# Starting a group's expert layer beside the dispatch of its second sequence, at a fixed pace

## The chip, the cores and the metric

The kernel runs on one core of one Trainium2 chip. The metric is the device time of one execution in microseconds (us), the median of the runs. TensorE is PE in the profile, its weight loads PEld, VectorE DVE, ScalarE ACT, GpSimd POOL and SyncE SP.

## The reference

The input is 16 sequences of 512 positions with 256 channels, all in fp32. Two layers follow each other, each with a residual and a layer norm.

The first layer is a selective state-space layer that runs in both directions. Each sequence is projected to 512 inner channels, convolved over 4 positions, and gives step sizes `dt` and, for each of 16 states, rows B and C. Per state and channel a running sum over the positions follows:

```
dA_cum = exp(reverse cumulative sum of dt * A)
xs = cumsum(dt * u * B * dA_cum) / (dA_cum + 1e-12)
y = sum over the 16 states of xs * C,  plus u * D
```

The two directions are added, gated by silu of a second projection, and projected back to 256 channels.

The second layer is a soft mixture of 16 experts with 64 slots each, 1024 slots in all:

```
logits = layernorm(x) @ slot embeddings
slots  = softmax over the positions (dispatch), applied to layernorm(x)
eout   = (gelu(slots @ Wg + bg) * (slots @ Wu + bu)) @ Wd + bd     for each expert
out    = softmax over all slots (combine), applied to eout
```

An expert's weights are three matrices of 512 KB.

## The kernel before, in words

**The scan sets the beat.** The loop at L1048 goes over the 16 sequences `b`. For each it calls `scan_part` four times (forward and backward, for two pairs of channel blocks of 128). A `scan_part` walks over the states in twos and, for each, over two channel blocks: 16 steps, so 64 steps for a sequence. A step has this work:

- POOL multiplies `du` by the B rows into `db` (L442), and at the end `hg` by the C rows `cs` (L471).
- ACT makes the decays `h` (L459) and the factors `th` (L461).
- DVE runs the scan (L465, L467) and joins it with `th` into `hg` (L470).
- PE adds `hg` up over the states by transposing it into the PSUM tile `acc` (L386), two steps later (`add_up`).

`hg` has four buffers, the rows `bs` and `cs` three; SP loads them. Some states, chosen by `diag_of`, let PE make `db` instead (`hd`, L420): four of 16 in the sequences 0 to 2, two of 16 after.

**Side work is threaded between the steps.** Everything else is written as Python generators, which hand out *pieces*: a few matmuls into one or two of three PSUM banks (`BANKS`), then, a step later, what empties the bank. There are three queues of generators, objects of the class `Side`:

- `prep` prepares the next scan part (projections, convolution, `dt`, transposes).
- `front` runs `finish(b)`: output projection, residual and layer norm of a finished sequence, then its `dispatch` (logits `pl`, softmax, transposes `pd`, slots `pq`, `sl`). Slots go to HBM (`s_dram`) in four quarters; `dispatched[b]` counts them.
- `back` runs `experts(g, 0, 8)` and then `combine` for both sequences of group `g`, the sequences 2g and 2g+1. `experts` works in eight pairs of experts, each pair on the slots of both sequences: the load `st<-s_dram`, gate matmuls `pg`, up `pu`, down `peo`, and the store `e_dram<-eo`. `combine` works in four blocks of 128 positions: logits again (`cl`), softmax, transposes (`ctp`), and `cpo`.

After each step `beside_scan` lets `prep` put in a piece, then `front` and `back` by credit:

```
            def paced_piece(self, gaps):
                self.credit = min(self.credit + sum(x[0] for x in self.gens) / max(self.left, 1), 2.0)
                self.left -= 1
                if self.credit >= 1.0 and self.piece(gaps):
                    self.credit -= 1.0
```

So a queue's pace is its pieces that remain by the steps that remain. `experts` already waits at each pair until its quarter of the second sequence's slots is there (`while not ready(ep): yield WAIT`); where the group starts late, it never has to.

**When a group starts.** In an odd sequence `b` from 3 on, the group g = (b - 3) / 2 joins `back`: both of its sequences were dispatched by then. It has 128 steps, the rest of this sequence and the next; group 6 joins in sequence 15 and has 64. In sequence 15 (`hurry`) pieces may follow each other without a gap. Group 7 has no scan beside it: after the last step comes a tail, in which `side_by_side` runs the last `finish`, what is left of `back`, and group 7, with eight PSUM banks.

The order within an engine is not always that of the source: the framework schedules by priority, and `late` pins an instruction to the program's order.

Of the kernel before, what the change touches and what calls it, by code (L numbers as in the profile page):

```python
# [55 lines left out]
def seq_layers(tc, ident, neghalf, a, out):  # L56
# [21 lines left out]
    nb = a["x"].shape[0]  # L78
    with ExitStack() as ctx:
# [200 lines left out]
        def diag_of(b):  # L280

            return (3, 7, 11, 15) if b < 3 else (5, 13)
# [124 lines left out]
        def scan_part(b, r, p, v, accs, done, then):  # L407

            prep.drain()
            prep.gens += [[1, g] for g in [turn_pair(b, r, p, v)] + then]  # L410
            w, ds = side[r], diag_of(b)
            made = {}

            def by_diagonal(n, c):

                diags.append(count[0])
                made[n, c] = h = bank(f"hd_{b}_{r}_{n}_{c}")
                for lc in range(NL):
                    s = slice(lc * P, (lc + 1) * P)
                    ins = nc.tensor.matmul(h[:, s], v[c][3][:, s], dg[:, s], start=True, stop=True)  # L420
                    if lc == 0:
                        late(ins)

            chunks = (2 * p, 2 * p + 1)
            for n in range(0, NS, 2):
                q = f"{b}_{r}_{p}_{n}"
                k = 1 if n + 1 in ds else 2

                bs = p4.tile([P, 2, L], F32, tag="bs", name=f"bs_{q}")
                cs = p4.tile([P, 2, L], F32, tag="cs", name=f"cs_{q}")  # L430
                nc.sync.dma_start(bs[:, :k, :], v["bc"][0, n : n + k, :].unsqueeze(0).to_broadcast([P, k, L]))
                nc.sync.dma_start(cs, v["bc"][1, n : n + 2, :].unsqueeze(0).to_broadcast([P, 2, L]))
                if n + 3 in ds:
                    dg = p4.tile([P, L], F32, tag="dg", name=f"dg_{q}", bufs=1)
                    nc.sync.dma_start(
                        dg.rearrange("p (l s) -> p l s", l=NL),
                        diag_dram[r, ds.index(n + 3), :, : P * P].rearrange("l (p s) -> p l s", p=P),
                    )
                for c in chunks:
                    dt, rr, du = v[c][:3]  # L440
                    db = p4.tile([P, 2, L], F32, tag="db", name=f"db_{q}_{c}")
                    nc.gpsimd.tensor_tensor(  # L442
                        db[:, :k, :], du.unsqueeze(1).to_broadcast([P, k, L]), bs[:, :k, :], ALU.mult
                    )
                    hg = p4.tile([P, 2, L], F32, tag="hg", name=f"hg_{q}_{c}", bufs=4)
                    hs = {}
                    for j in range(2):
                        if j < k:
                            dec = h = ps_h.tile([P, L], F32, tag="h", name=f"h_{q}_{c}_{j}")
                            hs[j] = (h, dec, db[:, j, :])  # L450
                        else:
                            h = made.pop((n + j, c))
                            dec = p4.tile([P, L], F32, tag="dec", name=f"dec_{q}_{c}", bufs=2)
                            hs[j] = (h, dec, h)

                    ths = {}
                    for j in range(2) if k == 2 else (1, 0):
                        s = slice(n + j, n + j + 1)
                        nc.scalar.activation(hs[j][1], dt, AF.Exp, scale=w["A"][:, c, s])  # L459
                        ths[j] = p4.tile([P, L], F32, tag="th", name=f"th_{q}_{c}_{j}")  # L460
                        nc.scalar.activation(ths[j], rr, AF.Tanh, bias=LN_1E12 / 2, scale=w["Ah"][:, c, s])  # L461
                    for j in range(2):
                        (h, dec, add), th = hs[j], ths[j]
                        if r == 0:
                            nc.vector.tensor_tensor_scan(h, dec, add, 0.0, ALU.mult, ALU.add)  # L465
                        else:
                            nc.vector.tensor_tensor_scan(  # L467
                                h[:, ::-1], dec[:, ::-1], add[:, ::-1], 0.0, ALU.mult, ALU.add
                            )
                        nc.vector.scalar_tensor_tensor(hg[:, j, :], th, 1.0, h, ALU.add, ALU.mult)  # L470
                    nc.gpsimd.tensor_tensor(hg, hg, cs, ALU.mult)  # L471
                    pending.append(
                        (r == n == 0, n == 0, r == 1 and n == NS - 2, c, hg, accs, w, v["u"], f"acc_{q}_{c}", done)
                    )
                    evict()

                    nxt_n = n if c == chunks[0] else n + 2
                    if nxt_n + 1 in ds:
                        for x in sides:
                            x.take_up()  # L480
                        by_diagonal(nxt_n + 1, chunks[1] if c == chunks[0] else chunks[0])
                    beside_scan()
                    if k == 1:
                        diags.pop(0)
                    add_up(2)

        class Side:


            def __init__(self):  # L490
                self.gens, self.hold, self.need, self.left, self.credit = [], None, 0, 0, 0.0
                self.wait = self.took = self.gap = False

            def add(self, steps, gen):
                self.gens.append([steps, gen])

            def begin(self, scan_steps):
                self.left, self.credit = scan_steps, 0.0
# [20 lines left out]
            def piece(self, gaps=True):  # L519

                done = False
                while self.gens and self.hold is None and not self.wait:
                    if self.gap and self.took and gaps:
                        break
                    oldest = min([x.hold for x in sides if x.hold is not None] + diags[:1], default=count[0])
                    if count[0] - oldest + self.need > BANKS:
                        break
                    done = True
                    head = self.gens[0]
                    head[0] = max(head[0] - 1, 1)  # L530
                    fresh = len(head) == 2
                    if fresh:
                        head.append(True)
                    self.go()
                    if not fresh and (not self.gens or self.gens[0] is head):
                        break
                return done

            def paced_piece(self, gaps):
                self.credit = min(self.credit + sum(x[0] for x in self.gens) / max(self.left, 1), 2.0)  # L540
                self.left -= 1
                if self.credit >= 1.0 and self.piece(gaps):
                    self.credit -= 1.0

            def drain(self):
                while self.gens:
# [4 lines left out]
        hurry = False  # L551
        diags = []

        prep, front, back = sides = [Side(), Side(), Side()]
# [480 lines left out]
                yield WAIT  # L1035
                put(0, NL, *both)

        FINISH, COMBINE, PAIR = 32, 14, 4
        fwd = {}
        prep.add(1, prep_forward(0, 0, ND, fwd))  # L1040
        prep.drain()
# [6 lines left out]
        for b in range(nb):  # L1048
            bwd, nxt, accs = {}, {}, {}

            if b >= 3 and b % 2 == 1:
                g = (b - 3) // 2
                back.add(8 * PAIR, experts(g, 0, 8))
                back.add(COMBINE, combine(2 * g))
                back.add(COMBINE, combine(2 * g + 1))
            hurry = b + 1 == nb
            front.begin(64)
            back.begin(128 if b % 2 == 1 and b + 1 < nb else 64)

            def gate(c, b=b, accs=accs, bwd=bwd):  # L1060
                y = bwd["res"]
                late(nc.vector.tensor_tensor(y[:, c, :], y[:, c, :], accs[c], ALU.mult))
                if c == ND - 1:
                    front.add(FINISH, finish(b, y))

            scan_part(
                b, 0, 0, fwd, accs, None, [turn_back(b, fwd, bwd), prep_backward(b, bwd), prep_pair(b, 1, 0, bwd)]
            )
            scan_part(b, 1, 0, bwd, accs, gate, [prep_gate(b, fwd, bwd), prep_pair(b, 0, 1, fwd)])
            then = [prep_pair(b, 1, 1, bwd)]  # L1070
            if b + 1 < nb:
                then.append(prep_forward(b + 1, 0, 2, nxt))
            scan_part(b, 0, 1, fwd, accs, None, then)
            then = [prep_forward(b + 1, 2, ND, nxt), prep_pair(b + 1, 0, 0, nxt)] if b + 1 < nb else []
            scan_part(b, 1, 1, bwd, accs, gate, then)
            front.drain()
            fwd = nxt
# [16 lines left out]
        g, kept = nb // 2 - 1, {}  # L1094
# [52 lines left out]
```

## Time and profile before

| what | value |
|---|---|
| median of 3 runs | 5326.35 us (5323.48 to 5327.91) |
| the profiled execution | 5322.25 us, its span 5320.5 us |
| mean granted PE clock | 0.897 |
| sequences 1 and 2 | 283.3 and 285.6 us |
| sequences 3 and 4 | 321.5 and 308.5 us |
| sequences 9 and 10 | 327.0 and 307.9 us |
| sequence 15 | 370.3 us |
| after the last step | 240.5 us |
| `s_dram<-sl`, issue to landing | 3.9 us |
| `st<-s_dram`, issue to landing | 4.2 us |

A sequence's time is taken from its first L471 product to the next sequence's first, and read with the stage windows. The odd sequences from 5 to 13 are alike, and so are the even ones from 4 to 14. The busy time of an engine is an average over stages with different limits, so it is read within one stage.

### The profile page before, as it was taken

What the parts mean: (1) busy time and instruction counts of PE and PEld (TensorE: products, weight loads), DVE (VectorE), ACT (ScalarE), POOL (GpSimd) and SP (SyncE); (2) the same over time, 40 slices, a digit from 0 to 9 for tenths busy, and PEclk for the clock granted to TensorE, in tenths of its full rate; (3) what the DMA queues carried; (4) which work ended last, traced back from release to release, by engine and by line L of the source; (5) the groups of instructions that cost most, each with busy time, mean ns of one, the idle gap of its engine ahead of it and who ended that gap; (6) DMA issues with size and microseconds to landing.
All of it is one profiled execution on the core that took longest, in us unless ns stands there. A gap on an engine that the chain in (4) does not pass through costs nothing. (4 is left out here: it accounts for less than half of the span.)

```text
span 5320.5 us, 74550 instructions
## 1 busy us (share of the span) xinstructions
PE 4310.4 (81%) x24498; PEld 3411.1 (64%) x24498; DVE 4560.6 (86%) x6284; ACT 4104.9 (77%) x6573; POOL 4681.6 (88%) x2537
## 2 busy tenths in 40 slices
PE   5677776897778978788788878889787897878889
PEld 3556565676567756676666766667666676657667
DVE  7999999889998899888898888988898889987733
ACT  6777878887888877888887887888778887777644
POOL 6999999989999899999999989998999989988710
PEclk7778888998899989999899988899888998889999
DMA  5444444675446644576446754467544664447545
GB/s 141 137 129 152 126 142 131 211 234 152 146 146 224 222 144 143 171 226 206 132 140 198 236 169 151 134 210 230 157 151 144 217 227 149 144 153 230 168 135 168
DMA packets 614820, 907.82 MB, mean 171 GB/s; under 512 B 84606, under 2 KB 404734, under 8 KB 614432
## 3 DMA queue, kind: packets, MB, share of 16 engines
q1 hardware_dynamic: 532740, 859.35, 50.9%
q10 hardware_dynamic: 81692, 43.70, 3.1%
q8 instruction: 195, 3.19, 0.2%
q14 instruction: 193, 1.58, 0.1%
HBM read 840.34 MB, written 62.56 MB: 170 GB/s over the span
## 5 line engine op out<-in xcount | busy, mean ns | idle before, releaser
L471 POOL TENSOR_TENSOR hg<-hg,cs 128x1024 f32<-128x1024 f32 x1024 | 2416.9, 2364 | 125.0 <-DVE hg L470 108.0
L442 POOL TENSOR_TENSOR db<-du,bs 128x1024 f32<-128x1024 f32 (+1 forms) x1024 | 2087.7, 2042 | 227.8 <-DVE h L465 84.1
L470 DVE SCALAR_TENSOR_TENSOR hg<-th,h 128x512 f32<-128x512 f32 x1744 | 1156.8, 679 | 183.4 <-PE acc L386 105.9
L386 PE MATMUL acc<-ident,hg 128*128 128x128 f32 x8192 | 1163.6, 292 | 106.4 <-POOL hg L471 84.6
L386 PEld LDWEIGHTS acc<-ident,hg 128*128 128x128 f32 x8192 | 1034.4, 152 | 284.6 <-POOL hg L471 131.3
L467 DVE TENSOR_TENSOR_SCAN h<-h,db 128x512 f32<-128x512 f32 x872 | 1044.9, 1219 | 104.9 <-ACT h L459 92.6
L465 DVE TENSOR_TENSOR_SCAN h<-h,db 128x512 f32<-128x512 f32 x872 | 1044.1, 1219 | 44.5 <-ACT h L459 43.6
L461 ACT ACTIVATE th<-rr,Ah_f 128x512 f32<-128x512 f32 x1024 | 724.6, 714 | 200.9 <-DVE hg L470 198.1
L461 ACT ACTIVATE th<-rr,Ah_b 128x512 f32<-128x512 f32 x1024 | 721.3, 712 | 153.5 <-DVE hg L470 143.5
L459 ACT ACTIVATE h<-dt,A_f 128x512 f32<-128x512 f32 x872 | 591.4, 680 | 99.5 <-DVE hg L470 96.3
L459 ACT ACTIVATE h<-dt,A_b 128x512 f32<-128x512 f32 x872 | 592.3, 680 | 85.6 <-DVE hg L470 81.7
L420 PE MATMUL hd<-dg,duT 128*128 128x128 f32 x2432 | 375.7, 305 | 73.2 <-ACT duT L364 27.1
L420 PEld LDWEIGHTS hd<-dg,duT 128*128 128x128 f32 x2432 | 347.9, 220 | 84.5 <-ACT duT L364 29.5
L710 PE MATMUL pl<-x2T,seT 128*128 128x512 f32 x512 | 294.1, 704 | 78.4 <-DVE hg L470 37.4
L838 PE MATMUL peo<-Wd,ht 128*128 128x256 f32 x1024 | 258.1, 408 | 63.2 <-DVE rr L346 36.6
L869 PEld LDWEIGHTS pg<-st,Wg 128*128 128x128 f32 x2048 | 243.1, 195 | 94.1 <-issue 82.8
L811 PE MATMUL pu<-st,Wu 128*128 128x128 f32 x2048 | 255.6, 284 | 49.3 <-DMA Wu<-in_Wu_dram 27.0
L1015 PE MATMUL cpo<-ceo,ct 128*128 128x256 f32 x1024 | 256.0, 407 | 43.2 <-DVE rr L346 40.0
L811 PEld LDWEIGHTS pu<-st,Wu 128*128 128x128 f32 x2048 | 245.9, 199 | 60.6 <-DVE h L467 29.5
L838 PEld LDWEIGHTS peo<-Wd,ht 128*128 128x128 f32 x1024 | 205.5, 206 | 106.1 <-DVE rr L346 39.2
L869 PE MATMUL pg<-st,Wg 128*128 128x128 f32 x2048 | 265.0, 284 | 4.5 <-DMA st<-s_dram 3.4
L1015 PEld LDWEIGHTS cpo<-ceo,ct 128*128 128x128 f32 x1024 | 207.2, 207 | 87.2 <-DVE rr L346 42.7
(165 smaller groups left out, 6754.0 us busy)
## 6 DMA issues: line engine op xcount, KB each, us to landing
cs<-bc SPq DMA_DIRECT2D x512, 512.0 KB, 3.9
bs<-bc SPq DMA_DIRECT2D x360, 512.0 KB, 5.2
Wg<-in_Wg_dram SPq DMA_DIRECT2D x128, 512.0 KB, 5.7
Wu<-in_Wu_dram SPq DMA_DIRECT2D x128, 512.0 KB, 5.8
Wd<-in_Wd_dram SPq DMA_DIRECT2D x128, 512.0 KB, 5.5
dg<-diag_dram SPq DMA_DIRECT2D x152, 256.0 KB, 4.3
bs<-bc SPq DMA_DIRECT2D x152, 256.0 KB, 3.5
x<-in_x_dram SPq DMA_DIRECT2D x32, 512.0 KB, 6.5
```

Of the source, the lines that this page charges most:

```text
L386: ins = nc.tensor.matmul(accs[c][:, s], hc[:, j, s], ident, is_transpose=True, start=False, stop=(last and j == 1 and lc == NL - 1),)
L420: ins = nc.tensor.matmul(h[:, s], v[c][3][:, s], dg[:, s], start=True, stop=True)
L442: nc.gpsimd.tensor_tensor(db[:, :k, :], du.unsqueeze(1).to_broadcast([P, k, L]), bs[:, :k, :], ALU.mult)
L459: nc.scalar.activation(hs[j][1], dt, AF.Exp, scale=w["A"][:, c, s])
L461: nc.scalar.activation(ths[j], rr, AF.Tanh, bias=LN_1E12 / 2, scale=w["Ah"][:, c, s])
L465: nc.vector.tensor_tensor_scan(h, dec, add, 0.0, ALU.mult, ALU.add)
L467: nc.vector.tensor_tensor_scan(h[:, ::-1], dec[:, ::-1], add[:, ::-1], 0.0, ALU.mult, ALU.add)
L470: nc.vector.scalar_tensor_tensor(hg[:, j, :], th, 1.0, h, ALU.add, ALU.mult)
L471: nc.gpsimd.tensor_tensor(hg, hg, cs, ALU.mult)
L811: nc.tensor.matmul(pu[:, fc * P : (fc + 1) * P], got["Wu", e][:, k, fc * P : (fc + 1) * P], st[:, k, :, j * SL : (j + 1) * SL], start=(k = ...
L838: nc.tensor.matmul(po[:, j * DM : (j + 1) * DM], ht[:, fc, :], got["Wd", e0 + j][:, fc, :], start=(fc == 0), stop=(fc == NF - 1),)
L869: nc.tensor.matmul(pg[:, fc * P : (fc + 1) * P], got["Wg", e][:, k, fc * P : (fc + 1) * P], st[:, k, :, j * SL : (j + 1) * SL], start=(not ...
```

## The change

A group joins `back` one sequence earlier, in the even sequence b = 2g + 2, while the dispatch of its second sequence (2g + 1) runs in `front`. The pairs start as the quarters of the slots are written. The pace of `back` is no longer worked out from what remains: it is 0.5 credits a step (`rate`), and a piece costs 1.1 credits in `experts` and 0.8 in `combine` (`weight`, the third entry of a generator's record). In the last sequence the old rule is put back, with 64 steps to go. Group 6 so starts in sequence 14, and group 7 is run in the tail as before. `diag_of` is not changed.

```diff
             def __init__(self):
+                self.rate = None
...
-            def add(self, steps, gen):
-                self.gens.append([steps, gen])
+            def add(self, pieces, gen, weight=1.0):
+                self.gens.append([pieces, gen, weight])
...
-                    fresh = len(head) == 2
+                    fresh = len(head) == 3
...
             def paced_piece(self, gaps):
-                self.credit = min(self.credit + sum(x[0] for x in self.gens) / max(self.left, 1), 2.0)
+                rate = self.rate or sum(x[0] for x in self.gens) / max(self.left, 1)
+                self.credit = min(self.credit + rate, 2.0)
                 self.left -= 1
+                weight = self.gens[0][2] if self.gens else 0.0
                 if self.credit >= 1.0 and self.piece(gaps):
-                    self.credit -= 1.0
+                    self.credit -= weight
...
-        FINISH, COMBINE, PAIR = 32, 14, 4
+
+        FINISH, COMBINE, EXPERTS = 32, (13, 0.8), (25, 1.1)
+        back.rate = 0.5
...
-            if b >= 3 and b % 2 == 1:
-                g = (b - 3) // 2
-                back.add(8 * PAIR, experts(g, 0, 8))
-                back.add(COMBINE, combine(2 * g))
-                back.add(COMBINE, combine(2 * g + 1))
+            if b >= 2 and b % 2 == 0:
+                g = b // 2 - 1
+                back.add(EXPERTS[0], experts(g, 0, 8), EXPERTS[1])
+                for i in range(2):
+                    back.add(COMBINE[0], combine(2 * g + i), COMBINE[1])
             hurry = b + 1 == nb
             front.begin(64)
-            back.begin(128 if b % 2 == 1 and b + 1 < nb else 64)
+            if hurry:
+                back.rate = None
+                back.begin(64)
```

More of the change, by code (lines that the diff above doesn't have):

```diff
@@ L409, in scan_part @@
             prep.drain()
-            prep.gens += [[1, g] for g in [turn_pair(b, r, p, v)] + then]
+            prep.gens += [[1, g, 1.0] for g in [turn_pair(b, r, p, v)] + then]
             w, ds = side[r], diag_of(b)
```

## The prediction

> **What bounds the kernel now.** I read the page first: no engine is near full over the whole span, and the page's chain of waits covers only the last few per cent, so the span has to be cut by sequence. Each sequence makes 64 `hg`-by-`cs` products on POOL (L471), so the first product of each marks its start; the stage windows between those marks are the next view.
>
> ```profile
> PE 4310.4 (81%) x24498; PEld 3411.1 (64%) x24498; DVE 4560.6 (86%) x6284; ACT 4104.9 (77%) x6573; POOL 4681.6 (88%) x2537
> ...
> core 0: us, PE busy (x) PEld busy (x) DVE busy (x) ACT busy (x) POOL busy (x), PEclk, DMA share, GB/s
> ...
> 619.20:762.40 143.20, 102.51 (x601) 84.11 (x600) 131.61 (x165) 112.24 (x180) 139.46 (x81) 0.82 0.44 135
> 762.40:904.80 142.40, 100.42 (x567) 80.00 (x566) 132.27 (x162) 116.76 (x186) 138.35 (x74) 0.84 0.43 138
> ...
> 2804.50:2968.20 163.70, 133.67 (x842) 112.35 (x839) 140.24 (x195) 131.69 (x201) 150.09 (x85) 0.92 0.65 206
> 2968.20:3131.50 163.30, 149.91 (x899) 118.31 (x899) 143.91 (x204) 129.84 (x198) 145.21 (x73) 0.97 0.69 222
> 3131.50:3286.10 154.60, 118.09 (x639) 92.20 (x639) 142.25 (x195) 124.84 (x209) 148.31 (x81) 0.86 0.45 139
> 3286.10:3439.40 153.30, 125.77 (x642) 92.42 (x641) 139.76 (x191) 123.74 (x209) 146.80 (x77) 0.91 0.44 142
> 4709.70:4898.90 189.20, 156.91 (x964) 128.36 (x961) 145.91 (x212) 143.16 (x213) 150.33 (x85) 0.90 0.65 206
> 4898.90:5080.00 181.10, 154.63 (x867) 121.48 (x868) 137.06 (x203) 121.84 (x204) 135.29 (x67) 0.95 0.52 166
> 5080.00:5320.50 240.50, 216.87 (x1216) 177.37 (x1215) 71.71 (x199) 97.36 (x210) 14.78 (x45) 0.97 0.52 160
> ```
>
> The rows are the halves of sequences 2, 9, 10 and 15, then the tail. Sequence 2, with no experts or combine beside it, is POOL's (278 us busy of 286). Sequence 9 has a whole group's experts (16, run as eight pairs): POOL works 295 us of 327. Sequence 10 has that group's combine (eight blocks of 128 rows): the same POOL work in 308 us. So experts cost about 9 us more per half than combine does. Sequence 15 has all of group 6's experts and most of its combine in its own 64 steps: 370 us, with less POOL work (286 us). How POOL is held up there is in the waits of its second half, and in the timeline of the tail's start, where TensorE is the busy engine:
>
> ```profile
> POOL hg L471 <- DVE hg L470: 26.4, 14, 4.6
> PEld ctp L954 <- ACT cm L947: 20.6, 9, 6.6
> PE ctp L954 <- ACT cm L947: 17.8, 5, 6.4
> DVE hg L470 <- PE acc L386: 11.8, 8, 4.8
> ...
> 5114.25 3.60 PE L933 MATMUL cl<-seT,cx 128*128 128x512 f32 x8
> 5119.63 1.32 PE L954 MATMUL ctp<-ident,cm 128*128 128x128 f32 x8 [1.79 <-ACT cm L947]
> 5120.79 0.60 PE L686 MATMUL px<-ident,xn 128*128 128x128 f32 x4
> 5121.23 3.66 PE L1015 MATMUL cpo<-ceo,ct 128*128 128x256 f32 x16
> ...
> 5150.60 5.42 PE L869 MATMUL pg<-st,Wg 128*128 128x128 f32 x32 [3.45 <-DMA st<-s_dram]
> ```
>
> Side matmuls that wait (`ctp` on ACT) hold back the `acc` transposes; those free the `hg` buffers (four) that DVE writes and POOL multiplies. The last rows also show one combine block still in the tail, between the two `px` transposes that the last sequence's dispatch needs.
>
> **The change, part by part.** The built order of the changed kernel holds the same matmuls; ScalarE's table loads rise from 346 to 349 (3 x 1.28 us on an engine that is 77% busy: nothing on the path). In sequences 3 to 14 it puts half a group's experts in the second half of an even sequence, the other half in the first half of the next odd one, and the combine in the halves between. The density stays what it was: about one pair or one block per eight steps.
>
> *Sequences 3 to 14.* Before, a pair of sequences is 163.7 + 163.3 + 154.6 + 153.3 = 634.9 us. The halves depend on what runs beside them and hardly on which half it is (163.7 against 163.3; 154.6 against 153.3). After, a pair is 163.7 + 154 + 154 + 163.3: the same sum. I take 0, with a gain of 14 us (bursts: the order no longer has stretches with four gate groups in eight steps) to a loss of 14 us (1 us a sequence) as bounds.
>
> *The first pair of each group.* It now waits for slots written just before. In the built order, `pg` of pair 0 stands two scan steps behind the `pq` that makes its slots; the later pairs stand eight steps or more behind theirs, which is cover. Two steps are 2 x 163.3/32 = 10.2 us, less `pq` itself 3.6: 6.6 us. The chain from `pq` to `pg` is `sl` on ACT (1.02), the store `s_dram<-sl` (3.9 to landing on the page) and the load `st<-s_dram` (4.2): 9.1 us. In the tail, with fewer transfers about, the same chain took 5.6 us (`pq` ended at 5145.0, `pg` began at 5150.6). So the wait is 0 to 2.5 us in each of seven groups; behind it on TensorE stand the next `acc` transposes. I take 1 us (two of the four `hg` buffers' worth of slack lies between): +7, bounds 0 and +21. The load also heads SP's queue while the store lands: behind it are `cs` and `bs` of the scan, issued three buffers ahead (two state pairs, some 20 us), which covers 4 us. If that cover were gone, POOL would wait those 4 us: the same bound again.
>
> The Trainium skill speaks against such a wait: TensorE: Matmul & The Clock Gate, "Step-by-step: what each phase is for", has matmuls stay in program order, only weight loads pulled ahead. The rows agree in kind (DVE held by `acc` for 11.8 us above). [...]
>
> *Sequence 2.* Its second half now carries four pairs. Before: 142.4. POOL there has 138.4 us of work (four diagonals instead of two), and beside experts a half runs 163.3 - 145.2 = 18.1 us over POOL's: 156.5, so +14. Bounds: combine's excess of 6.5 us (+2.5), and the whole 163.3 (+21), since this sequence has twice as many `hd` matmuls.
>
> *Sequence 15.* The order leaves it four pairs and nearly all the combine. TensorE's prices are 2 x (1.12 + 2.05) for a pair's gate, 3.74 up, 3.62 down, and 3.60 + 1.3 + 3.62 = 8.5 for a combine block. First half: before 10 gate, 10 up, 5 down = 68.5 us for 189.2; the usual first half beside experts 54.9 for 163.7; after 8, 8, 5 and half a block's scores = 62.1. On the line between them: 177. Second half: before 77.3 us of side work for 181.1; usual combine 34 for 153.3, less 11.5 of POOL work (the next sequence's preparation isn't there) = 141.8; after 55.9, on the line 162. Sum 339 against 370.3: -31. Bounds: -45 (325, like an ordinary odd sequence) and -15 (the uncapped hurry, in which pieces follow each other without a gap, remains).
>
> *Tail.* One block of sequence 13's combine is left instead of three: two blocks, 17 us of TensorE. But the front's own chain (`pyt`, `po`, moments, factors, `xn`, `px`) runs beside them: from the last `po` at 5109.5 to the first `px` at 5120.8 it is 11.3 us. Without the blocks `po` ends some 3.5 us earlier, `xn` isn't queued behind a `cm` on ACT, and the second `px` not behind `cpo` (3.66): -7.5, bounds -4 and -17.
>
> Sum: 0 + 7 + 14 - 31 - 7.5 = -17.5. The profiled execution took 5322.25 (span 5320.5): 5304.8. The median of the three runs is 4.1 above it: 5309, which I give as 5310.
>
> **The rivals.**
>
> *Slower: the fresh slots stall TensorE and SP.* Place: the first `pg` of seven groups and the `st` load ahead of it. For it: 9.1 us of chain against 6.6 of cover; before, SP once waited 12.7 us for that store. Against: the tail's 5.6. At 12.7 - 6.6 = 6.1 us each it is 43 instead of 7: 5346. Without any wait the sum is -24.5, so it turns to slower by 0.2% from 5 us a group.
>
> *No change.* Sequence 2 costs its whole 21, sequence 15 gives 15, the tail 4, the waits 7: +9; with the small gain of steadier steps about 0. Time 5327.
>
> *Much faster: mixing pays.* Excess over POOL is 12.8 us for 68 us of side work (sequence 10), 31.7 for 110 (sequence 9) and 85 for 146 (sequence 15): a curve. If only a sequence's sum counted, a half-and-half sequence would save 5.8 us against the chord, 69 in twelve. Against: the halves above don't mix within themselves, and four `hg` buffers remember some 20 us, not 150. Two thirds of it: 5265.
>
> **How the numbers follow.** A measurement of this kernel can tell 0.2% from no change, some 10.7 us. Forecast (5295 to 5325) 0.48, slower 0.20, no change 0.18, mixing 0.14. Of the forecast 0.40 lies below 5315.7. Faster: 0.40 + 0.14 = 0.54. Same: 0.08 + 0.16 = 0.24. Slower: 0.20 + 0.02 = 0.22. The range takes the rivals' near parts: 5270 to 5350; the forecast's own is 5295 to 5325.
>
> **What would show it.** In the profile after: sequences 3 to 14 at about 317 us each, not 327 and 308; sequence 2 at 300, sequence 15 at 340, the tail at 233. `pg` waiting for `st<-s_dram` should be under 10 us in all outside the tail. Wrong if sequences 3 to 14 move by over 1 us each, or sequence 15 stays over 356: the pieces' lack of a gap would then be its cost, not their number.

## The result: 4% slower, all of it in sequences 3 to 14

| what | before | after | forecast |
|---|---|---|---|
| median (4 runs each) | 5326.94 us | 5536.66 us (5532.91 to 5539.89) | 5310 |
| ratio, 95% interval | | 1.0395 [1.0377, 1.0413] | |
| span of the profiled execution | 5320.5 us | 5536.9 us | |
| mean granted PE clock | 0.897 | 0.882 | |
| sequence 2 | 285.6 us | 301.2 us | 300 |
| sequences 3 to 14, sum | 3805.0 us | 4056.1 us | 3805 to 3812 |
| sequence 15 | 370.3 us | 331.7 us | 339 |
| after the last step | 240.5 us | 229.2 us | 233 |

As before, a sequence is timed from its first L471 product to the next one's. Sequence 2, sequence 15 and the tail came out near the forecast, 34 us better together (24.5 were forecast); the middle lost 251 us. The page's first part shows no engine with more work:

```profile
PE 4420.4 (80%) x24498; PEld 3489.6 (63%) x24498; DVE 4573.4 (83%) x6284; ACT 4104.6 (74%) x6576; POOL 4683.7 (85%) x2537
```

DVE, ACT and POOL are busy within 13 us of before, with the same instructions but for three more on ACT. So for these three the 216 us of span are idle time. (PE is busy for 110 us more with the same 24498 matmuls; its granted clock is 0.882 in place of 0.897.) The stage windows place it; the rows are the second half of sequence 2, the halves of 9, 10 and 15, and the tail:

```profile
761.90:919.90 158.00, 139.67 (x845) 111.67 (x845) 137.95 (x183) 126.67 (x194) 138.78 (x73) 0.94 0.65 205
2943.70:3118.90 175.20, 142.72 (x849) 116.76 (x846) 146.54 (x204) 130.20 (x200) 148.60 (x81) 0.86 0.64 204
3118.90:3289.60 170.70, 143.86 (x714) 108.53 (x714) 140.20 (x196) 125.56 (x210) 146.96 (x76) 0.89 0.44 135
3289.60:3453.60 164.00, 121.19 (x655) 94.66 (x656) 146.09 (x199) 126.08 (x211) 148.26 (x81) 0.86 0.40 127
3453.60:3625.20 171.60, 145.25 (x801) 113.02 (x800) 136.16 (x184) 128.89 (x198) 146.99 (x77) 0.88 0.59 195
4976.00:5147.40 171.40, 140.90 (x894) 117.81 (x892) 147.40 (x211) 135.49 (x205) 148.56 (x81) 0.94 0.65 213
5147.40:5307.70 160.30, 134.62 (x694) 102.24 (x693) 132.45 (x190) 117.14 (x206) 134.99 (x67) 0.92 0.37 115
5307.70:5536.90 229.20, 202.22 (x1152) 167.35 (x1150) 66.35 (x185) 92.60 (x198) 14.60 (x44) 0.95 0.53 166
```

Sequences 9 and 10 were to take 163.7 + 154 + 154 + 163.3. They take 175.2 + 170.7 + 164.0 + 171.6: every half is 8 to 17 us over, those that hold mostly combine too, with POOL's work unchanged (148.6 and 147.0 us against 150.1 and 145.2). The halves of 15 (171.4 and 160.3) and the tail are as worked out. A line of the waits in the second half of 15, and group 7's first gate on TensorE in the tail, answer to the lines shown of before:

```profile
POOL hg L471 <- DVE hg L470: 14.6, 6, 5.4
```

```profile
5365.79 6.85 PE L872 MATMUL pg<-st,Wg 128*128 128x128 f32 x32 [3.27 <-DMA st<-s_dram]
```

POOL's wait for `hg` there falls from 26.4 to 14.6 us, and group 7's gate begins 58.1 us after the last step (5365.8 less 5307.7), before 70.6 (5150.6 less 5080.0).

Where the middle loses it, the costliest groups say first. These are DVE's `hg` and the gate after, then the `hg` of before; idle time stands last:

```profile
L470 DVE SCALAR_TENSOR_TENSOR hg<-th,h 128x512 f32<-128x512 f32 x1744 | 1156.7, 677 | 325.4 <-PE acc L386 144.1 <-ACT th L461 122.8 <-POOL hg L471 12.1
...
L872 PE MATMUL pg<-st,Wg 128*128 128x128 f32 x2048 | 292.4, 302 | 37.7 <-DMA st<-s_dram 37.4
```

```profile
L470 DVE SCALAR_TENSOR_TENSOR hg<-th,h 128x512 f32<-128x512 f32 x1744 | 1156.8, 679 | 183.4 <-PE acc L386 105.9 <-ACT th L461 39.4 <-ACT et L725 0.8
```

DVE waits longer for the `acc` transposes (+38) and above all for ACT's factors `th` (39.4 to 122.8). The gate waits 37.4 us for its slots, before 3.4: the rival of the fresh slots is there, but far too small for 251.

### The profile page after: what moved, and what is told of

The parts are those of the page before. It is cut to its first block, busy times and chain, and to the rows that moved or that the text cites. A ratio compares the mean times of both kernels' runs of the same rounds, so it can differ in the third digit from the quotient of the medians.

```text
span 5536.9 us, 74558 instructions
## 1 busy us (share of the span) xinstructions
PE 4420.4 (80%) x24498; PEld 3489.6 (63%) x24498; DVE 4573.4 (83%) x6284; ACT 4104.6 (74%) x6576; POOL 4683.7 (85%) x2537
## 5 line engine op out<-in xcount | busy, mean ns | idle before, releaser
L471 POOL TENSOR_TENSOR hg<-hg,cs 128x1024 f32<-128x1024 f32 x1024 | 2416.2, 2363 | 151.0 <-DVE hg L470 91.4
L470 DVE SCALAR_TENSOR_TENSOR hg<-th,h 128x512 f32<-128x512 f32 x1744 | 1156.7, 677 | 325.4 <-PE acc L386 144.1
L386 PE MATMUL acc<-ident,hg 128*128 128x128 f32 x8192 | 1176.0, 294 | 102.5 <-POOL hg L471 85.7
L386 PEld LDWEIGHTS acc<-ident,hg 128*128 128x128 f32 x8192 | 1045.7, 154 | 271.6 <-POOL hg L471 113.1
L872 PEld LDWEIGHTS pg<-st,Wg 128*128 128x128 f32 x2048 | 268.8, 212 | 136.2 <-issue 79.3
L872 PE MATMUL pg<-st,Wg 128*128 128x128 f32 x2048 | 292.4, 302 | 37.7 <-DMA st<-s_dram 37.4
L713 PE MATMUL pl<-x2T,seT 128*128 128x512 f32 x512 | 262.3, 638 | 61.0 <-ACT th L461 24.5
L936 PE MATMUL cl<-seT,cx 128*128 128x512 f32 x480 | 248.8, 667 | 61.2 <-DVE rr L346 31.8
L749 PE MATMUL pq<-dis,xn 128*128 128x256 f32 x1024 | 254.4, 405 | 17.9 <-DVE hg L470 8.4
```

Of the source, the lines that this page charges most:

```text
L386: ins = nc.tensor.matmul(accs[c][:, s], hc[:, j, s], ident, is_transpose=True, start=False, stop=(last and j == 1 and lc == NL - 1),)
L872: nc.tensor.matmul(pg[:, fc * P : (fc + 1) * P], got["Wg", e][:, k, fc * P : (fc + 1) * P], st[:, k, :, j * SL : (j + 1) * SL], start=(not ...
```

## The experiments

"3 to 14" is the sum of those twelve sequences, 3805.0 before and 4056.1 after. Where no interval is given, a kernel was timed once; the kernel before took 5324.65, 5333.10, 5326.24 and 5330.97 us in the single runs beside them.

### One part of the change at a time

**old_start_new_pace**: the constant pace alone; groups join in odd sequences as before.

```diff
-            if b >= 2 and b % 2 == 0:
-                g = b // 2 - 1
+            if b >= 3 and b % 2 == 1:
+                g = (b - 3) // 2
```

> Groups start in the odd sequences again, as before; the constant pace of 0.5 and the weights of the change stay. Theory F (fresh slots: the wait for just-written slots stalls TensorE and SP): the steady pair of sequences comes back to 635 us, whole time about 5310. Theory S (start: experts beside the second half of a sequence and combine beside its first half go badly with the rest of the side work): the same, 635 and 5310. Theory P (pace: fixed credits that run full make pieces collide): the steady pair stays near 675, time above 5500.

Measured: 5391.93 us; 3 to 14: 3885.1 (+80).

**new_start_old_pace**: the early start alone; the pace is worked out from what remains, as before.

```diff
-        FINISH, COMBINE, EXPERTS = 32, (13, 0.8), (25, 1.1)
-        back.rate = 0.5
+        FINISH, COMBINE, EXPERTS = 32, (14, 1.0), (32, 1.0)
...
-            if hurry:
-                back.rate = None
-                back.begin(64)
+            back.begin(128 if b % 2 == 0 else 64)
```

> Groups start in the even sequences as in the change; the pace is worked out again from the pieces and steps that remain (128 from the start, 64 in the second sequence), weight 1. Theory P: the steady pair comes back to 635, and with the gains at the ends the time is about 5290. Theories F and S: the pair stays near 675, time about 5530.

Measured: 5375.21 us; 3 to 14: 3886.6 (+82). Both lie between the times that the theories named. Neither part makes 251 alone, and the pace costs 80 without any early start. That run does hold 36 more table loads on ACT (6609 instructions against 6573), some 46 us of its time, so the 80 need not be positions alone.

**stale_slots**: the experts load the slots of the group before, so the load never waits for a store just made. The order of the engines is kept.

```diff
-                        s_dram[b0 : b0 + 2, k, :, ep * 2 * SL : (ep + 1) * 2 * SL].rearrange("b p s -> p b s"),
+                        s_dram[max(b0 - 2, 0) : max(b0 - 2, 0) + 2, k, :, ep * 2 * SL : (ep + 1) * 2 * SL].rearrange("b p s -> p b s"),
```

> The changed kernel, but the slots that experts load are those of the group before (group 0 its own), so the load never waits for a store of the last steps; the outputs are those of other slots. Theory F: the steady pair falls to 635 to 640, time about 5300. Theories P and S: it stays at 670 or more, with only the 5.3 us per group that the gate waited for the load gone; time 5490 to 5540.

Measured: 5514.44 us; 3 to 14: 4036.0, so by these two runs the fresh slots cost 20 of the 251. `pg` no longer waits for `st` at all.

**quarter_later**: a pair may begin only when one more quarter of the slots is written.

```diff
-                return dispatched.get(b0 + 1, 0) > ep // 2
+                return dispatched.get(b0 + 1, 0) >= min(ep // 2 + 2, 4)
```

> The changed kernel, but each expert pair waits for one quarter of the slots more than its own, so the group begins about ten steps later and no slot is fresh. Theory F: steady pair 635 to 640, time about 5300. Theory S: part of the loss goes, pair 650 to 665, time 5400 to 5480. Theory P: no change, pair near 675, time about 5530.

Measured: 5394.41 us; 3 to 14: 3894.2 (+89). Much more comes back than the 20 us that slots cost: moving the pieces does something of its own.

### Which engine's pieces are on the path

Three cuts leave out a part of each expert, in the kernel after and, as control, in the one before. First DVE's multiply of the up projection, one of four blocks kept:

```diff
-                for fc in range(NF):
+                for fc in range(1):
```

> The changed kernel with only the first of the four multiplications by the up result per expert (128 of 512 rows), so VectorE has 16 us less per group, 98 us in sequences 3 to 14; the experts' output is not the reference's. Theory B: VectorE's bunches fall from 735 to 525, and sequences 3 to 14 lose 200 us or more, to 3800 to 3860; time 5290 to 5340. If VectorE isn't what holds the steps: a loss of at most 98 us, time above 5435.

> The same cut in the kernel before, as the control. Theory B: VectorE's bunches fall from 583 to 427, but POOL's work of 295 us a sequence is near; sequences 3 to 14 lose 60 to 130 us, time 5190 to 5265. If VectorE's bunches play no part, both kernels lose the same.

Measured: after 5458.09 us, 3 to 14: 3975.9 (80 less, where theory B wanted 200 or more); before 5265.66 us, 3748.9 (56 less). So DVE's pieces are not the whole cause.

Then ScalarE's: tanh in place of gelu, which needs no load of another function table.

```diff
-                    args = (ht.rearrange("p f s -> p (f s)"), pg, AF.Gelu)
+                    args = (ht.rearrange("p f s -> p (f s)"), pg, AF.Tanh)
```

> The changed kernel with tanh for gelu in the scan-side experts and the tail's (the output is not the reference's): the scan's exp and tanh need no other table, so ScalarE loses the table loads around each pair's gelu, some 20 us a group, 125 in sequences 3 to 14. Theory A (ScalarE: its side work now falls where the next factor is due; VectorE's idle time ended by ScalarE in sequences 3 to 14 rose from 168 to 353 us): sequences 3 to 14 lose 150 us or more, from 4056 to below 3906, and VectorE's wait for ScalarE falls to 250 or less. Theory O (order: side matmuls stand in TensorE's queue ahead of their inputs, whatever their length): at most 60 us, above 3996.

> The same cut in the kernel before, as the control. Theory A: at most 60 us of 3805 in sequences 3 to 14, since ScalarE's lateness is small there. Theory O: the same as in the changed kernel, within 25 us.

Measured: after 5359.26 us, 3 to 14: 3894.2 (162 less); before 5281.07 us, 3764.0 (41 less). In sequences 3 to 14 the table loads fall from 264 to 144 and from 260 to 144, at 1.283 us each 154 and 149 us of ACT's time. Before, little more than a quarter of that was won; after, all of it and 8 us more. Theory A's second mark was missed: VectorE's waits for ScalarE there stay at some 270 us, not 250. Nor is it the amount alone: without the loads the pieces move too (in sequence 4 the up matmuls begin at steps 42, 49 and 57, in the kernel after at 41, 49 and 56).

Last TensorE's: two of four down matmuls.

```diff
-                    for fc in range(NF):
+                    for fc in range(NF // 2):
```

> The changed kernel with two of the four down matmuls of each expert left out (half of the inner channels; the output is not the reference's): TensorE loses 14.5 us a group, 87 in sequences 3 to 14. Theory A: little, up to 40 us, as with VectorE's cut, since the down piece isn't what ScalarE waits for. Theory T (TensorE is the bound after the change): 87 us or more, below 3970.

> The same cut in the kernel before, as the control. Theories A and T: up to 40 us of 3805 in sequences 3 to 14.

Measured: after 5480.38 us, 3 to 14: 4009.4 (47 less, just over theory A's 40 and far under theory T's 87); before 5331.87 us, 3825.3 (20 more). All three engines' pieces count for more after than before. After the change, taking away work on any of them helps; in the kernel before, less TensorE work went with 20 us more, in its one run. Amounts don't explain that; positions may.

### Where the pieces fall

**rate_045** and **combine_weight_09** change only the pace, `back.rate = 0.45` and `COMBINE = (13, 0.9)`. Their expectations come from a count in the built orders: how much side work of DVE and ACT bunches in windows of three steps.

> The changed kernel with 0.45 credits a step instead of 0.5, nothing else. Theory B (bunches: the pace sets which side pieces of front, back and prep fall into the same three steps, and VectorE and ScalarE have too little slack there): counted in the built order over sequences 3 to 14, VectorE's side work above 1.1 us a step in windows of three steps is 583 us before, 735 in the change and 617 here; ScalarE's above 2.0 us a step 401, 467 and 467. The four kernels run so far lie on about 1.17 us per us of the first and 0.8 of the second, so sequences 3 to 14 take 3805 + 40 + 53 = 3900, plus up to 20 for fresh slots, and the whole 5390 to 5420. Theory S (the early start itself): no gain, sequences 3 to 14 near 4050, time 5520 to 5540.

> The changed kernel with a weight of 0.9 instead of 0.8 for combine's pieces, nothing else. Theory B: the count stays high (VectorE 742, ScalarE 446), so sequences 3 to 14 take about 3805 + 186 + 36 + 20 = 4047 and the whole about 5530, although combine is slowed like the rate of 0.45 slows it. A theory that any slower pace helps: near 5400.

Measured: 5385.79 us with 3 to 14 at 3887.5, and 5525.44 us with 4039.8. Both sums lie within 13 us of the count's 3900 and 4047; the first total is 4 us under its range.

Next the first pair of each group waits a fixed number of steps more; order, weights and pace of the pieces stay:

```diff
                 while not ready(ep):
                     yield WAIT
+                for _ in range(1 if ep == lo and g + 1 < nb // 2 else 0):
+                    yield WAIT
```

> The changed kernel, but the first pair of each group's experts waits one step more before its first piece; order of pieces, pace and weights are kept, so every piece of back stands one step later beside the pieces of prep and front. Theory phase (the loss is made where pieces of back fall into the same steps as DVE and ACT pieces of prep and front): the built order still bunches DVE's side work as in the changed kernel (724 us over 1.1 us a step in windows of three steps, against 735 after and 583 before), so sequences 3 to 14 stay slow: 3980 to 4060 us (after 4056), total 5460 to 5540. Theory placement (experts beside a dispatch cost more, wherever the single pieces stand): 4040 to 4075, within 20 of after. This run alone doesn't tell the two apart; with the next one it does.

> The changed kernel with the same wait of three steps in place of one; pieces, order, pace and weights kept. Theory phase: the built order now bunches as little as the kernel before (586 us against 583), ScalarE's a bit more (531 against 401), so sequences 3 to 14 fall by 100 to 180 us, to 3880 to 3960, and the total to 5360 to 5440, though half of each group's experts still stand beside a dispatch. Theory placement: three steps of 64 move hardly anything from one half to another, so 4036 to 4076 and a total over 5515.

Measured: one step 5512.86 us, 3 to 14: 4026.6; three steps 5424.51 us, 3902.1. Both lie where the positions were said to decide. But the second sum tells the two theories apart less than its text says: at a constant pace the delays add up, and from group 3 on the experts begin only at step 57 of the even sequence, nearly all of them in the odd one again. Two of the 48 pairs of these sequences also fall to sequence 15, which takes 371.9 us in place of 331.7.

Sequence 4 is free of this. It has the up and down matmuls of the same three pairs and the same combine blocks in all these kernels; the pairs' steps differ (where their up matmuls begin, by the trace). The fourth pair's gate stands in steps 62 and 63, in delay_three_steps it falls to sequence 5; steps 60 to 64 take 18.6 us in all four.

| kernel | pairs at steps | steps 0 to 40 | 40 to 44 | 48 to 52 | sequence 4 |
|---|---|---|---|---|---|
| after | 41, 49, 56 | 203.4 | 30.0 | 24.2 | 337.1 |
| stale_slots | 41, 49, 56 | 203.5 | 25.2 | 23.9 | 331.4 |
| delay_one_step | 43, 50, 56 | 203.3 | 22.2 | 24.4 | 330.9 |
| delay_three_steps | 44, 53, 61 | 203.3 | 20.0 | 18.5 | 322.1 |

The first 40 steps agree within 0.2 us. Then three pairs moved by three to five steps give back 15.0 us, of which at most 5.7 are the fresh slots. new_start_old_pace says it too: its sequences 8 and 10 have four pairs beside the dispatch and take 311.9 and 311.5 us. So experts beside a dispatch needn't be dear; at these steps they are.

The timeline shows what happens in steps 40 to 44 of the kernel after: TensorE first, then DVE, then POOL.

```profile
1456.29 0.80 PE L872 MATMUL pg<-st,Wg 128*128 128x128 f32 x2 [5.14 <-DMA st<-s_dram]
1457.02 2.07 PE L867 MATMUL pg<-ident,bg_rows 64*128 64x512 f32 x2
1459.02 5.84 PE L872 MATMUL pg<-st,Wg 128*128 128x128 f32 x30
1464.70 1.04 PE L386 MATMUL acc<-ident,hg 128*128 128x128 f32 x8
```

```profile
1465.85 0.69 DVE L470 SCALAR_TENSOR_TENSOR hg<-th,h 128x512 f32<-128x512 f32 x1 [6.15 <-PE acc L386]
...
1473.38 0.74 DVE L204 SCALAR_TENSOR_TENSOR xf<-pin,cw_f,xf 128x511 f32<-128x511 f32 x1
1474.04 1.22 DVE L465 TENSOR_TENSOR_SCAN h<-h,db 128x512 f32<-128x512 f32 x1
1475.17 0.72 DVE L204 SCALAR_TENSOR_TENSOR xf<-pin,cw_f,xf 128x510 f32<-128x510 f32 x1
1475.81 0.68 DVE L470 SCALAR_TENSOR_TENSOR hg<-th,h 128x512 f32<-128x512 f32 x1
1476.40 0.74 DVE L204 SCALAR_TENSOR_TENSOR xf<-pin,cw_f,xf 128x509 f32<-128x509 f32 x1
1477.06 2.15 DVE L826 SCALAR_TENSOR_TENSOR ht<-pu,bu_cols,ht 128x128 f32<-128x128 f32 x8
1479.13 2.33 DVE L465 TENSOR_TENSOR_SCAN h<-h,db 128x512 f32<-128x512 f32 x2
```

```profile
1468.90 1.28 POOL L442 TENSOR_TENSOR db<-du,bs 128x512 f32<-128x512 f32 x1 [6.73 <-issue]
...
1480.48 4.69 POOL L442 TENSOR_TENSOR db<-du,bs 128x1024 f32<-128x1024 f32 x2 [4.09 <-issue]
```

Two hits follow each other. The gate waits 5.14 us for its slots and then runs slowly: the granted clock is 0.50 around it, and its two bias matmuls take 2.07 us where the prediction's price was 1.12.

```profile
1453.50:1463.70 10.20, 7.41 (x26) 5.68 (x27) 5.88 (x9) 5.05 (x7) 8.67 (x4) 0.50 0.44 154
```

The `acc` transposes stand behind the gate on TensorE: DVE is idle for 6.15 us, and POOL for 6.73. The profile names no releaser for POOL ("issue"), but the scan that reads an earlier `db` ends at 1468.76, 0.14 us before POOL goes on. Then the convolution taps `xf` of `prep` (2.20 us in three) and the pair's `ht` (2.15), pieces of two queues, fall between the same scans: DVE is busy without a gap, and POOL, the engine that bounds this stage, stands for 4.09 us more. With three steps of delay these taps have ended at 1470.5 us, before the up matmuls begin at 1477.6, and the same four steps take 20.0 us. The window's rows, after and then delay_three_steps:

```profile
1459.80:1489.80 30.00, 25.73 (x159) 21.61 (x158) 22.52 (x34) 19.18 (x31) 18.88 (x11) 0.88 0.49 160
```

```profile
1460.20:1480.20 20.00, 17.60 (x118) 13.77 (x117) 17.00 (x22) 18.67 (x28) 16.51 (x10) 0.99 0.58 183
```

### The ring of buffers

Five `hg` buffers in place of four, paid for by two `bs` in place of three, in both kernels.

```diff
-                bs = p4.tile([P, 2, L], F32, tag="bs", name=f"bs_{q}")
+                bs = p4.tile([P, 2, L], F32, tag="bs", name=f"bs_{q}", bufs=2)
...
-                    hg = p4.tile([P, 2, L], F32, tag="hg", name=f"hg_{q}_{c}", bufs=4)
+                    hg = p4.tile([P, 2, L], F32, tag="hg", name=f"hg_{q}_{c}", bufs=5)
```

> The changed kernel with five hg buffers in place of four, paid for in space by two bs buffers in place of three. Theory ring (a late add-up on TensorE holds DVE through the four hg buffers; in the sequences 9 and 10 DVE waits 22.2 us for acc after, 13.8 before): the extra buffer takes away most of these waits, six pairs of sequences by some 15 us or more, so 3 to 14 fall by 60 to 130 us, to 3925 to 3995. Theory serial (ScalarE's and DVE's own side work delays the scan's steps, and TensorE is only late because of them): at most 30 us less, or more time by the missing bs buffer: 4025 to 4080.

> The kernel before with the same five hg and two bs buffers, as the control. Theory ring: gains no more than 13.8 us a pair of sequences, and about half of that is likely, since its waits for acc are short (9.4 us in the second half of sequence 9, 9 times): 3 to 14 at 3740 to 3790 (before 3805). Theory serial: 3790 to 3830.

Measured: after 5506.58 us, 3 to 14: 4010.6 (45 less); before 5370.48 us, 3857.1 (52 more). The first lies between the two expectations, the control outside both: in the kernel before, the two edits together cost time. The fifth `hg` buffer did what was meant (DVE's whole wait for `acc` falls from 144.1 to 32.1 us after, and from 105.9 to 76.2 before), and the gap between the kernels shrinks from 251 to 153 us. That speaks for a part played by the four buffers. But the two edits can't be separated, and the pieces move with them (in sequence 5 of the kernel after, up matmuls from steps 8 and 25 to 10 and 26), so its size stays open.

### The best positions found

The two orders with the least bunching that an early start gave: `back.rate = 0.45` with the wait above over two, or five, steps.

> The changed kernel at 0.45 credits a step and with a wait of two steps ahead of each group's first pair: of the variants whose orders were built, one of the two in which the pieces of the three queues collide least (DVE's bunches 617 us, ScalarE's 411; the kernel before 583 and 401). Theory phase, with the line fitted to the earlier runs (0.8 us for each us of ScalarE's bunches over before, 1.17 for DVE's): 48 us over before in sequences 3 to 14, 3853, give or take 25; with the 34 us that sequence 2, sequence 15 and the tail give, the total is 5326 + 48 - 34 = 5340 (5315 to 5365), so it would about equal the kernel before. Theory placement (an early start costs its 82 us whatever the phase): 3885 or more, total 5372 or more.

> The same with a wait of five steps in place of two: DVE's bunches 583 us, as before, ScalarE's 458. Theory phase: 46 us over before in sequences 3 to 14, 3851, give or take 25, total 5338 (5313 to 5363). Theory placement: 3885 or more, total 5372 or more.

Measured: two steps 5366.17 us, ratio 1.0071 [1.0056, 1.0086], 3 to 14: 3870.9 (+66), sequence 15 at 352.4; five steps 5397.39 us, 1.0126 [1.0109, 1.0143], 3875.0 (+70), sequence 15 at 372.2. In the middle both are within what positions were said to give, and better than 3885. The totals miss, the first by 1 us, because a slower pace leaves more for sequence 15, which gives 18 us or nothing where the change as made gave 39. No version with the whole computation beat the kernel before.

## Why the prediction was wrong

**The step that failed** is "The halves depend on what runs beside them and hardly on which half it is", and from it "the same sum. I take 0", with 1 us a sequence for a bound. It measured 251 us, 21 a sequence. That 163.7 agreed with 163.3 and 154.6 with 153.3 showed only that before's positions suit both halves. It was no evidence for other positions, and the change moves every piece: before, the up matmuls of the odd sequences (from 5 on) began at steps 8, 16, 24, 32 and so on; after, at 1, 8, 15, 25, 33, and 41, 49, 56 in the even ones. Two queues that each keep a density of one pair per eight steps can still meet in the same step every time, and then they meet in all six groups. A wider bound would have come from rows in which pieces do crowd, such as sequence 15 of before (with more work in it): its first half takes 189.2 us beside 150.3 of POOL work. What the runs showed instead is that positions count: in sequence 4 the same three pairs, three to five steps later, take 15.0 us less, and over sequences 3 to 14 another order of the same early start takes 185 us less.

**The first pair** was put at 1 us a group. By the trace the six gates in question wait 5.14, 6.53, 4.29, 5.94, 6.59 and 5.17 us, and stale_slots prices them at some 20 us. That is just inside the bound of 21, which doesn't follow from its own terms (0 to 2.5 us in each of seven groups is at most 17.5). The tail's 5.6 us weighed too much there: if the chain took its 9.1 us, waits of 5.6 on the mean leave a cover of 3.5, not of 6.6. The rival had the wait's size nearly right (6.1) but not its price (43). The Trainium skill, TensorE: Matmul & The Clock Gate, "Step-by-step: what each phase is for", has matmuls stay in program order; the `acc` at 1464.70 above, behind a gate that waited, fits it.

**What held.** Sequence 2: +15.6 against +14. Sequence 15: -38.6 against -31, with halves of 171.4 and 160.3 where the line between usual halves gave 177 and 162. The tail: -11.3 against -7.5. Their sum is -34.3 against -24.5. In these the stage's load changed, and it was read from rows of that load; sequences 3 to 14 kept their load and changed only positions.

**No rival had this case.** "Mixing pays" looked at a sequence's sum as well, and had the wrong sign.

**What is shown, and what stays open.** Shown: some 20 us are fresh slots; neither start nor pace is the cause alone; leaving out 154 us of ACT's table loads gives 162 back after, and leaving out 149 gives 41 before; in sequence 4 a shift of the same three pairs by three to five steps moves 15.0 us. And 185 of the 251 us (251 less 66, the 20 of the slots among them) go with other positions and a slightly lower pace, at the same early start; 21 of these 185 come back in sequence 15. The count of bunched work said 3980 to 4060, 3880 to 3960, 3853 and 3851 for the orders with a delay, and 4026.6, 3902.1, 3870.9 and 3875.0 came out. Still it is only a mark of the cause: quartering DVE's pieces gave back 80 where that reading wanted 200 or more.

Open: the price of a single meeting, the odd sequences, whose steps weren't taken apart like those of sequence 4, and whether the last 66 us are positions too. Open too is TensorE's clock, which no run holds fixed. These rows are sequences 3 to 14, before and then after; the clock is the third number from the end:

```profile
904.80:4709.80 3805.00, 3162.18 (x18062) 2487.08 (x18063) 3394.22 (x4672) 3055.05 (x4868) 3541.18 (x1869) 0.91 0.56 178
919.90:4976.00 4056.10, 3282.68 (x18094) 2573.31 (x18093) 3409.93 (x4679) 3061.56 (x4880) 3545.11 (x1873) 0.89 0.53 167
```

TensorE is busy for 120 us more with all but the same matmuls. A loss doesn't need the lower clock: in the same stretch it is 0.91 in old_start_new_pace, new_start_old_pace and quarter_later, as before, and these lose 80 to 89 us. But the kernels that lose over 220 (after, stale_slots, delay_one_step, combine_weight_09) all have 0.89. Whether the lower clock adds to their loss or only follows from TensorE's waits wasn't tested.

As for the positions, some do nearly as well as those of before: in delay_three_steps the sequences 5 and 6 take 637.3 us and 7 and 8 take 640.4, against 634.9 before, with seven pairs of experts in each in place of eight.

## What to carry to other kernels

Where side work is threaded by steps beside an engine that is nearly full, its sum per stage alone need not set the time; here the steps at which pieces met counted too. Before a change of start or pace, list the steps at which each queue's pieces fall, and count it as a cost where two queues need the same engine in the same steps. A pace with a fixed period can bring such a meeting back in every group, as here; shifting all pieces by a few steps is a cheap first trial. Here it gave back a part of the loss and never the whole.

## What the runs showed of the hardware

A change of function table on ScalarE took 1.283 us as one instruction, and nothing else beside it: in the kernel after, `ht` (L898) ends at 1465.50, the load runs from 1465.51 to 1466.79, and the next exponential begins at 1466.81. The Trainium skill, ScalarE: Activation LUTs, "What ACT_TABLE_LOAD costs", has the same 1283 ns and a drain of some 1380 ns on top, which isn't visible here.
